# A depthwise convolution's band weights: two loads of the same rows, or one load and a ScalarE copy across partitions

## The chip, the cores and the metric

The program runs on one NeuronCore of a Trainium2 chip. The metric is the device time of one launch in microseconds (us), as a median over runs. PE is TensorE, PEld its weight loads, DVE is VectorE, ACT is ScalarE, POOL is GpSimd and SP is SyncE, which here only issues DMAs.

## The reference

Two layers act on an image batch `x` of 32 x 128 x 56 x 56 (images, channels, rows, columns), all in float32. Layer 0 is a ConvNeXt-like block with routed experts; layer 1 treats the pixels as tokens and does an attention within each token and a second routed feed-forward. Cut to what matters here, layer 0 begins with

```python
x = jax.lax.conv_general_dilated(input, dw_kernel, (1, 1), ((3, 3), (3, 3)),
        feature_group_count=C, dimension_numbers=('NCHW', 'OIHW', 'NCHW')) + dw_bias[None, :, None, None]
x = jnp.transpose(x, (0, 2, 3, 1))
...                      # layer norm over the channels, router, top 2 of 8 experts, expert MLPs
return input + x_skip + moe_out
```

So each channel is convolved with its own 7 x 7 kernel. The change touches only this first step. Everything behind it (router, selection, experts, the token attention, the second feed-forward) is the same in both kernels.

## The kernel before, in words

**The convolution as matmuls.** For one channel and one column offset `kw`, the 7 vertical taps are a banded 56 x 56 matrix that maps input rows to output rows. The kernel puts image rows on partitions and does, for each of the 128 channels, 7 offsets `kw` x 4 matmuls of 64 x 64 quadrants of the PE array: the upper partitions (0 to 55) hold images 0 to 15, the lower ones (64 to 119) images 16 to 31, and each half is cut in two groups of 8 images. That makes 28 matmul instructions for a channel; the profile has two records for each, 56 in all (L241).

**The bands.** A padded copy of all kernels is written once to a tensor `band_d` in device memory (L208). For channel `c`, a DMA with overlapping rows (row step one element) reads 56 rows of 728 elements of it into the tile `band` (L225). This is done twice, once for the upper and once for the lower partitions (`r` = 0, 1), with the same source. DVE then copies the 56 useful columns of each of the 7 offsets in reversed order into `br` (L235), over all 128 partitions. `br` holds the weights that the matmuls use: the upper half for `r = 0`, the lower half for `r = 1`. `band`, `br` and the input tile `xin` each have three buffers that channels take in turn, so the buffers of channel `c` are written again for channel `c + 3`.

**In and out.** Two DMAs on SP's queue load the channel's images into `xin` (L231). The results of the two halves stand in two PSUM tiles `cps`, of which there are four (two channels). ACT takes the first one out with a bias into `ot` (L253), DVE the second (L255), and four DMAs on ACT's queue store them to `conv_d` (L258). `ot` has four buffers, again two channels.

**What sets the order.** The kernel is written as a plain loop over channels. The framework orders the instructions of each engine's queue by its own estimate, and an engine runs its queue in that order. Eight semaphores are dealt out in turn to the DMAs of SP and ACT together; before a DMA is issued, its queue waits for the DMA that had the same semaphore before. In this kernel a channel has 8 such DMAs (2 `xin`, 2 `band`, 4 stores), so each of them gets the semaphore of its own kind of the channel before.

At the start a few small copies for the next stage stand among the convolution's instructions: in DVE's queue, `raw<-wg` (L342), which waits for the load of the router's weights `wg` (L333, issued by SP), stands between `br` of channel 5 and `ot` of channel 3. The next stage, the router, begins with loads of `conv_d` into `ct` (L358) and matmuls `pc<-jm,ct` (L364).

Of the kernel before, what the change touches and what calls it, by code (L numbers as in the profile page):

```python
# [20 lines left out]
KS = 7  # L21
# [4 lines left out]
def conv_attn_hybrid_kernel(  # L26
# [24 lines left out]
    nc = tc.nc  # L51
    N, C, H, W = x.shape
# [34 lines left out]
    band_d = dram.tile([C, KS * 2 * H], F32, name="band_d")  # L87
# [107 lines left out]
    HP = P // 2  # L195
    NB = NK // 2
    BL = (KS - 1) * 2 * H + H
    assert H <= HP and NK % 2 == 0 and NB * W * 4 <= 2048
    with tc.tile_pool(name="cv_c", bufs=1) as cc, tc.tile_pool(
        name="cv", bufs=3  # L200
    ) as cv, tc.tile_pool(name="cv_p", bufs=4, space=PSUM) as cvp:
        wt = cc.tile([C, KS, KS], F32, name="wt")
        nc.sync.dma_start(wt.rearrange("c a b -> c (a b)"), dw_kernel.rearrange("c o a b -> c (o a b)"))
        gp = cc.tile([C, KS, 2 * H], F32, name="gp")
        nc.vector.memset(gp, 0.0)
        for kh in range(KS):
            nc.vector.tensor_copy(gp[:, :, H - 1 - PAD + kh], wt[:, kh, :])
        nc.sync.dma_start(band_d, gp.rearrange("c a b -> c (a b)"))  # L208
        bias = cc.tile([P, C], F32, name="bias")
        nc.sync.dma_start(bias, dw_bias.partition_broadcast(P))  # L210

        nbuf = 3
        bands = [cc.tile([P, KS, 2 * H], F32, name=f"band{i}") for i in range(nbuf)]
        turned_bands = [cc.tile([P, KS, HP], F32, name=f"br{i}") for i in range(nbuf)]
        xins = [cc.tile([P, NK, WP], F32, name=f"xin{i}") for i in range(nbuf)]
        for i in range(nbuf):
            nc.vector.memset(bands[i], 0.0)
            nc.vector.memset(turned_bands[i], 0.0)
            nc.gpsimd.memset(xins[i], 0.0)
        cview = conv_d.rearrange("n c (h w) -> c h n w", w=W)  # L220
        for c in range(C):
            bt, br, xi = bands[c % nbuf], turned_bands[c % nbuf], xins[c % nbuf]
            for r in range(2):
                rows = slice(r * HP, r * HP + H)
                nc.sync.dma_start(  # L225
                    bt[rows].rearrange("p a b -> p (a b)")[:, :BL],
                    bass.AP(
                        band_d.tensor, band_d.offset + c * KS * 2 * H, [[1, H], [1, BL]]
                    ),
                )  # L230
                nc.sync.dma_start(  # L231
                    xi[rows, :, PAD : PAD + W],
                    x[r * NK : (r + 1) * NK, c].rearrange("n h w -> h n w"),
                )
            nc.vector.tensor_copy(br[:, :, :H], bt[:, :, :H][:, :, ::-1])  # L235
            pss = [cvp.tile([P, NB, W], F32, name="cps") for r in range(2)]
            for kw in range(KS):
                for r in range(2):
                    rows = slice(r * HP, r * HP + H)
                    for b in range(2):  # L240
                        nc.tensor.matmul(  # L241
                            pss[r][b * HP : (b + 1) * HP],
                            br[rows, kw, :],
                            xi[rows, b * NB : (b + 1) * NB, kw : kw + W],
                            start=(kw == 0),
                            stop=(kw == KS - 1),
                            tile_position=(r * HP, b * HP),
                            skip_group_check=True,
                        )
            for r in range(2):  # L250
                ot = cv.tile([P, NB, W], F32, name="ot", bufs=4)
                if r == 0:
                    nc.scalar.activation(ot, pss[r], AF.Identity, bias=bias[:, c : c + 1])  # L253
                else:
                    nc.vector.tensor_scalar(ot, pss[r], bias[:, c : c + 1], None, ALU.add)  # L255
                for b in range(2):
                    n0 = r * NK + b * NB
                    nc.scalar.dma_start(  # L258
                        cview[c][:, n0 : n0 + NB, :], ot[b * HP : b * HP + H]
                    )  # L260
# [553 lines left out]
    with tc.tile_pool(name="ex_w", bufs=2) as ew, tc.tile_pool(  # L814
# [42 lines left out]
        for i, (e, b) in enumerate(blocks):  # L857
# [15 lines left out]
            xa, rows, n = got.pop(i)  # L873
# [607 lines left out]
    with tc.tile_pool(name="f_c", bufs=1) as cc, tc.tile_pool(  # L1481
# [6 lines left out]
        rows = cc.tile([E2, FF2], F32, name="hbr")  # L1488
# [110 lines left out]
```

## Time and profile before

| | |
|---|---|
| median of 3 runs | 9506.17 us (9501.17 to 9524.23) |
| the profiled execution's own time | 9507.39 us |
| its span, first to last instruction | 9505.7 us |
| mean granted TensorE clock | 0.945 |
| the convolution's matmuls (L241), first and last start | 11.1 us and 700.6 us |
| their records, and the mean of one | 7168, 541 ns |
| DVE copy `br<-band` | 128 x 381 ns |
| ACT `ot<-cps` / DVE `ot<-cps` | 128 x 633 ns / 128 x 683 ns |
| bytes of one DMA: `xin`, `band`, store to `conv_d` | 196.0, 159.2, 98.0 KB |

The span is 1.7 us shorter than the execution's own time. A busy time is the sum of an engine's instruction durations; four quadrant matmuls run beside each other, so the 541 ns of one record is not the pace of the PE. An instruction's idle time is put down to what released it last. DMA issues and semaphore waits on a queue are not busy time of the engine, but the engine behind the queue can do nothing else meanwhile.

### The profile page before, as it was taken

To read this page: it belongs to the slowest core of one execution; us is meant where nothing else is said; L and a number is where in the kernel's file an instruction comes from. 1 tells how busy PE (TensorE), PEld (TensorE's weight loads), DVE (VectorE), ACT (ScalarE), POOL (GpSimd) and SP (SyncE) were. 2 spreads that over 40 slices of the span, in tenths; PEclk is the share of its full clock that TensorE was granted. 3 is DMA by queue.
4 is the path that set the end of the run, shared out by engine and by line. 5 is a ranking of instruction groups with operands and counts; after the bars stand their busy time and mean duration, and the time that the engine had idled before them with its cause. 6 is when DMAs were issued, how large, how long until landed. Compare 5 with 4: busy or idle time off the path is not lost. (4 is left out here: it accounts for less than half of the span.)

```text
span 9505.7 us, 165321 instructions
## 1 busy us (share of the span) xinstructions
PE 8565.6 (90%) x62216; PEld 6983.3 (73%) x62216; DVE 6481.0 (68%) x10957; ACT 5277.1 (56%) x13401; POOL 6777.5 (71%) x4884
## 2 busy tenths in 40 slices
PE   9999558775999999998999999999999999999878
PEld 3459546554766666666889899988989988989733
DVE  1117889885222222225999999999999999999623
ACT  1116644332333333334788888888888888888600
POOL 0002137777787777777999999999999999999500
PEclk9999779998999999999999999999999999999865
DMA  9994238775444444442000000000000000000199
GB/s 205 213 205 142 70 103 226 209 210 150 77 62 71 71 69 69 70 65 39 25 31 31 31 28 26 29 31 31 31 31 25 29 30 31 31 31 31 62 317 336
DMA packets 996146, 849.92 MB, mean 89 GB/s; under 512 B 525013, under 2 KB 880664, under 8 KB 975859
## 3 DMA queue, kind: packets, MB, share of 16 engines
q1 hardware_dynamic: 470162, 494.25, 18.6%
q0 software_dynamic: 177664, 188.81, 11.5%
q10 hardware_dynamic: 347520, 156.28, 6.1%
q8 instruction: 493, 8.08, 0.4%
q14 instruction: 307, 2.51, 0.1%
HBM read 486.34 MB, written 353.64 MB: 88 GB/s over the span
## 5 line engine op out<-in xcount | busy, mean ns | idle before, releaser
L161 POOL TENSOR_TENSOR s<-s,q 128x2048 f32<-128x2048 f32 x784 | 3601.9, 4605 | 137.8 <-DVE s L161 107.5
L161 ACT ACTIVATE s<-s 128x2048 f32<-128x2048 f32 x784 | 1500.8, 1914 | 685.9 <-POOL s L161 682.2
L161 POOL DMA_INDIRECT t_d<-ys,xe x992 | 1530.5, 1543 | 409.2 <-issue 229.0
L161 DVE TENSOR_TENSOR s<-kv,c 128x2048 f32<-128x2048 f32 x784 | 1786.5, 2279 | 8.0 <-POOL c L161 8.0
L161 DVE TENSOR_TENSOR ev<-s,kv 128x2048 f32<-128x2048 f32 x784 | 1784.0, 2276 | 2.4 <-ACT s L161 2.4
L161 PE MATMUL sm<-ident,ev 128*128 128x128 f32 x12544 | 1530.6, 276 | 45.4 <-DVE ev L161 45.4
L161 PE MATMUL sm<-ident,s 128*128 128x128 f32 x12544 | 1526.1, 275 | 8.5 <-ACT s L161 8.5
L161 PEld LDWEIGHTS sm<-ident,ev 128*128 128x128 f32 x12544 | 1436.3, 144 | 92.8 <-DVE ev L161 50.6
L161 PEld LDWEIGHTS sm<-ident,s 128*128 128x128 f32 x12544 | 1405.0, 143 | 20.8 <-ACT s L161 8.7
L888 ACT ACTIVATE hT<-ph,b1t 128x512 f32<-128x512 f32 (+1 forms) x992 | 679.3, 685 | 1236.5 <-PE ph L884 1220.8
L899 DVE TENSOR_TENSOR ys<-py,b2t 128x512 f32<-128x512 f32 (+1 forms) x248 | 171.4, 691 | 1545.9 <-PE py L894 1454.2
L894 PEld LDWEIGHTS py<-w,hT 128*128 128x128 f32 x7936 | 960.6, 192 | 202.1 <-issue 91.5
L894 PE MATMUL py<-w,hT 128*128 128x128 f32 x7936 | 984.6, 278 | 0.2
L884 PE MATMUL ph<-xeT,w 128*128 128x512 f32 (+1 forms) x1984 | 921.3, 597 | 69.5 <-DVE xeT L880 69.5
L697 POOL DMA_INDIRECT xb_d<-xs,rd x784 | 766.5, 978 | 240.2 <-issue 199.2
L241 PE MATMUL cps<-xin,br 56*64 56x448 f32 x7168 | 687.5, 541 | 13.6 <-DVE br L235 11.1
L884 PEld LDWEIGHTS ph<-xeT,w 128*128 128x128 f32 x1984 | 348.3, 190 | 392.0 <-issue 293.2
L241 PEld LDWEIGHTS cps<-xin,br 56*64 56x64 f32 x7168 | 334.0, 132 | 366.4 <-issue 331.2
L161 PE MATMUL pa<-rw,ct 128*128 128x256 f32 x1568 | 393.4, 393 | 127.6 <-DVE xs L161 127.5
L287 POOL MEMSET code<- 128x64 f32 x1 | 0.2, 151 | 697.4 <-DMA conv_d<-ot 697.4
L161 PEld LDWEIGHTS pa<-rw,ct 128*128 128x128 f32 x1568 | 283.7, 194 | 261.0 <-DVE xs L161 172.0
L161 PE MATMUL kv<-wq,zT 128*128 128x256 f32 x1568 | 417.2, 389 | 52.7 <-DVE ev L161 52.3
(330 smaller groups left out, 13264.5 us busy)
## 6 DMA issues: line engine op xcount, KB each, us to landing
ct<-conv_d SPq DMA_DIRECT2D x192, 448.0 KB
xin<-in_x_dram SPq DMA_DIRECT2D x256, 196.0 KB
conv_d<-ot ACTq DMA_DIRECT2D x512, 98.0 KB
t_d<-xs ACTq DMA_DIRECT2D x112, 448.0 KB
tr<-t_d SPq DMA_DIRECT2D x112, 448.0 KB
to<-t_d SPq DMA_DIRECT2D x32, 1568.0 KB
out_dram<-oo ACTq DMA_DIRECT2D x32, 1568.0 KB
xg<-in_x_dram SPq DMA_DIRECT2D x96, 448.0 KB
```

What stands on the lines that cost most here:

```text
L161: r = getattr(self.engine, name)(*a, **k)
L241: nc.tensor.matmul(pss[r][b * HP : (b + 1) * HP], br[rows, kw, :], xi[rows, b * NB : (b + 1) * NB, kw : kw + W], start=(kw == 0), stop=(kw ...
L287: nc.gpsimd.memset(code, -1.0)
L697: s = nc.gpsimd.indirect_dma_start(out=xb_d, out_offset=bass.IndirectOffsetOnAxis(ap=idx, axis=0), in_=row, in_offset=None, bounds_check=R ...
L884: nc.tensor.matmul(ph[:, :, :rows], w1[:, f * P : (f + 1) * P], xT[:, :, :rows], start=True, stop=True,)
L888: nc.scalar.activation(hT[:, f, :, :rows], ph[:, :, :rows], AF.Gelu, bias=b1t[:, f : f + 1])
L894: nc.tensor.matmul(py[:rows, j, :], hT[:, f, j, :rows], w2[:, f, :], start=(f == 0), stop=(f == NF - 1),)
L899: nc.vector.tensor_tensor(ys[:rows], py[:rows], across(b2t, SB)[:rows], ALU.add)
```

## The change

One band load for a channel instead of two, into the upper partitions alone. DVE reverses the upper half alone (56 partitions). ACT then copies the finished weights from the upper to the lower partitions of `br`.

```diff
         for c in range(C):
             bt, br, xi = bands[c % nbuf], turned_bands[c % nbuf], xins[c % nbuf]
+            nc.sync.dma_start(
+                bt[:H].rearrange("p a b -> p (a b)")[:, :BL],
+                bass.AP(band_d.tensor, band_d.offset + c * KS * 2 * H, [[1, H], [1, BL]]),
+            )
             for r in range(2):
                 rows = slice(r * HP, r * HP + H)
                 nc.sync.dma_start(
-                    bt[rows].rearrange("p a b -> p (a b)")[:, :BL],
-                    bass.AP(
-                        band_d.tensor, band_d.offset + c * KS * 2 * H, [[1, H], [1, BL]]
-                    ),
-                )
-                nc.sync.dma_start(
                     xi[rows, :, PAD : PAD + W],
                     x[r * NK : (r + 1) * NK, c].rearrange("n h w -> h n w"),
                 )
-            nc.vector.tensor_copy(br[:, :, :H], bt[:, :, :H][:, :, ::-1])
+            nc.vector.tensor_copy(br[:H, :, :H], bt[:H, :, :H][:, :, ::-1])
+            nc.scalar.copy(br[HP : HP + H, :, :H], br[:H, :, :H])
```

In the built program the new copy for channel `c + 3` stands in ACT's queue behind `ot` of channel `c` and its four stores, and ahead of `ot` of channel `c + 1`. In DVE's queue `br` of channel `c + 3` now stands ahead of `ot` of channel `c` instead of behind it. With seven DMAs for a channel, the eight semaphores no longer fall on the same kind of DMA in each channel. `raw<-wg` stands two channels earlier in DVE's queue, ahead of `ot` of channel 1, and SP issues the load of `wg` sooner. From the router on, each engine's instructions stand in the same order as before.

## The prediction

> **What bounds the kernel now.** The change touches only the convolution, so I read first when that stage runs and which engine sets its pace: the busy time by stretches, for the matmul line L241 alone. The columns are time, PE busy with its records, PEld busy with its records, granted clock, DMA share, GB/s.
>
> ```profile
> 0.00:50.00 50.00, 37.09 (x344) 14.88 (x348) 0.97 0.88 180
> 50.00:100.00 50.00, 50.00 (x532) 19.95 (x528) 1.00 1.05 213
> ...
> 250.00:300.00 50.00, 49.73 (x520) 22.11 (x516) 1.00 1.01 211
> 300.00:400.00 100.00, 99.57 (x1048) 47.74 (x1044) 1.00 1.04 215
> 400.00:500.00 100.00, 100.00 (x1056) 44.52 (x1052) 1.00 1.03 214
> 500.00:600.00 100.00, 100.00 (x1058) 72.79 (x1054) 1.00 1.04 213
> 600.00:700.00 100.00, 100.00 (x1056) 52.09 (x1048) 1.00 0.96 197
> ```
>
> Two things are full at once. PE runs 1056 records in 100 us at full clock; a channel has 56, so it takes 56 / 1056 x 100 = 5.30 us. The DMA engines show a share near 1.0: a channel moves 2 x 196.0 + 2 x 159.2 + 4 x 98.0 = 1102.4 KB, which at 213 GB/s takes also 5.30 us. Which one leads? In the last row the DMA rate falls to 197 GB/s and the record count stays 1056, so PE has a pace of its own. In the rows of 250 to 400 us the count falls a little (520 against 530 or so, 1048 against 1056): there DMA led for moments.
>
> All 128 channels at 5.30 us are 679 us. From the first matmul (11.1 us) to the end of the last (701.1 us) are 690. So about 11 us of the stage are not PE's pace: that is all that an edit to the feeding can remove behind the first matmul. The second view, who waited for whom up to 700 us, says why PE is so rarely held although the other engines wait all the time:
>
> ```profile
> PE cps L241 <- DVE br L235: 11.1, 1, 11.1
> PE cps L241 <- DVE ot L255: 1.8, 1, 1.8
> PE cps L241 <- DMA xin<-in_x_dram: 0.6, 3, 0.3
> ...
> ACT ot L253 <- DMA conv_d<-ot: 372.2, 79, 6.0
> ACT ot L253 <- PE cps L241: 224.4, 46, 13.3
> ```
>
> PE waited for the first weights (11.1 us), once for an eviction, and almost never for images. ACT waited 372 us for stores; that is slack, as long as it ends before PE needs the PSUM tile two channels on. The one long hold is on DVE, in the timeline at the start of the stage (start, duration, engine, line, and in brackets the idle time before):
>
> ```profile
> 33.38 0.39 DVE L235 COPY br<-band 128x392 f32<-128x392 f32 x1 [2.88 <-DMA band<-band_d]
> 42.03 0.17 DVE L342 COPY raw<-wg 128x8 f32<-128x8 f32 x1 [8.26 <-DMA wg<-in_L_conv_Wg_dram]
> 42.15 0.68 DVE L255 TENSOR_SCALAR ot<-cps,bias 128x448 f32<-128x448 f32 x1
> ```
>
> DVE stood 8.3 us for the router's small weight load; the eviction of channel 3 came behind it, and channel 5 could not go on. PE lost 2.3 us between two groups of matmuls, and in the 4 us after that the granted clock reads 0.57; channel 5 took 9.4 us instead of 5.3, so the hold costs 4.1 us.
>
> A rule on this can be set beside it: the Trainium skill, "TensorE: Matmul & The Clock Gate", Part 1, has the clock halve after an idle window of about 3.4 us. Here a hold of some 2.3 us was followed by a low clock, so the row decides; by the rule alone the hold would cost 2.3.
>
> **The change part by part**, against the profiled execution's own 9507.39 us (1.2 us above the median).
>
> *Removed: one `band` load a channel.* 128 x 159.2 KB and 128 issues of about 0.39 us on SP. At 213 GB/s it is 0.77 us of DMA time a channel, 98 us in all, but PE's 5.30 us stay, so what is won is only where DMA made PE late after start-up: the small holds between 250 and 370 us. The starts of the channels there are 0.3, 0.25, 0.16, 0.40, 0.59 and 0.40 us late: 2.1 us. I take -2.1; the bounds are -2.1 and 0.
>
> *Changed: DVE's reversal on 56 partitions.* Still 392 elements for a partition, so still 0.38 us: nothing. It now stands ahead of DVE's `ot` of three channels before. Both wait for the same channel of PE, and the band has landed long before (SP issues it right after the reversal three channels earlier, some 16 us ahead). So `ot` moves by 0.4 us with two channels of slack: nothing.
>
> *Added: 128 ACT copies, 56 x 392, SBUF to SBUF.* No row has this form. Near ones are the 448-element eviction at 0.633 us and the `pk<-m` copy of 14 elements out of SBUF at 0.198; on the line between them 392 elements take 0.58 us. The bounds are 0.46 (the fastest 384-element copy from PSUM) and 0.69 (the 512-element ACTIVATE); the eviction is the nearest row, so I take 0.58, with 0.1 for each handover.
>
> A price in the skill, "VectorE: DVE Perf Modes", section on the TRN2 errata, speaks against many small ScalarE copies out of SBUF (224 cycles before the first element) and gives (224 + 392) / 1.2 GHz = 0.51 us, as an estimate; only if all copies lay in the open would the sum differ, by 128 x 0.07 = 9 us.
>
> Where does it lie? Behind the four stores of channel c, ahead of `ot` of channel c + 1. This is ACT's queue where DMA was late, and where it was not (the ACTq rows are the stores' issues with the waits between them):
>
> ```profile
> 249.56 4.49 ACTq L258 DMA_DIRECT2D conv_d<-ot  x4
> 254.10 0.63 ACT L253 ACTIVATE ot<-cps,bias 128x448 f32<-128x448 f32 x1 [5.11 <-DMA conv_d<-ot]
> 255.27 4.80 ACTq L258 DMA_DIRECT2D conv_d<-ot  x4
> ```
> ```profile
> 150.40 0.63 ACT L253 ACTIVATE ot<-cps,bias 128x448 f32<-128x448 f32 x1 [4.68 <-PE cps L241]
> 151.06 3.84 ACTq L258 DMA_DIRECT2D conv_d<-ot  x4
> 155.72 0.63 ACT L253 ACTIVATE ot<-cps,bias 128x448 f32<-128x448 f32 x1 [4.68 <-DMA conv_d<-ot]
> ```
>
> In the easy stretch the last store is issued 4.4 us after PE ended the channel, and ACT is then free for 0.8 us (154.90 to 155.72): the copy of 0.58 and a handover fit. In the late stretch the last store goes out up to 7.5 us after PE's end. The copy then ends at 7.5 + 0.1 + 0.58 + 0.1 = 8.3 us, and PE starts channel c + 3 two channels after that end, at 10.6. It is hidden with 2.3 us to spare even there, and the next eviction comes 0.7 us later with the same two channels of slack. Nothing on the path; if the cover were gone it would be 0.68 a channel, 87 us.
>
> *The semaphores.* Each DMA still waits for the one eight back, which is now one channel and one DMA back. Stores wait in part for loads and the other way round. With eight DMAs in flight and seven for a channel, the round trip may take 8 / 7 x 5.30 = 6.1 us instead of 5.3 before PE feels it. Nothing, or the small gain counted above.
>
> *Start.* The second band load of channel 0 was issued 0.39 us after the first and is gone; the copy and a handover (0.68) come before the first lower matmul. +0.3; bounds -0.4 and +0.7.
>
> *The wait for `wg`.* The load stands earlier on SP, behind the band load that follows DVE's reversal for channel 3 (about 19.5 us). Issued by some 22 us and landed 3.8 us after that, as before (38.2 to 42.0), it is there at about 26; DVE's `ot` of channel 1 behind it is needed only when PE starts channel 3, at 29.5. So the hold goes: -4.1. If the loads ahead on SP make it 4 us later, a like hold comes two channels earlier: 0.
>
> *Behind the stage* the order is the same and the first `ct` load waits for the last stores; all of it moves with the end.
>
> Sum: -2.1 + 0.3 - 4.1 = -5.9 us, and 9507.39 - 5.9 = 9501.5; on the median, 9500.3. I forecast 9500. That is 0.06%; a measurement of this kernel tells about 0.3% (28 us) from no change.
>
> **Rivals.** *ACT's queue becomes the bound (slower).* In the late stretch `ot` to `ot` on ACT is already 5.5 to 6.0 us, with nothing in it but the eviction and the stores' waits. If these waits do not shrink when a load is gone, a copy of 0.58 with its handover makes the loop 0.68 longer. It decides once the loop is over 5.30 us for many channels in a row. In the some 30 channels from 205 to 370 us alone: 30 x 0.68 = 20 us, 9526. In all 128: 87 us, 9593. For it: 372 us of ACT's waits are for stores. Against it: these waits last as long as transfers are in flight, and 14% of the bytes go; most channels outside that stretch have ACT waiting for PE.
>
> *DMA was the bound underneath (faster).* If the equal 5.30 us of DMA were what paced PE, a channel would fall towards 4.53 us: up to 98 us, 9408. Against it: the count of records did not move between 197 and 215 GB/s, and PE's records stand without idle time. Even with every hold gone the stage ends 11 us sooner: 9495, no measurable gain.
>
> *The edit's gains do not show:* `wg` is late again and the late stretch stays. Then only the start's 0.3 is left: 9506 on the median.
>
> **How the numbers follow.** My forecast, and the rivals that end within 28 us of it (holds all gone, holds all kept, ACT's loop late in one stretch): 0.80. ACT's loop as the bound over most channels, 34 us and more: 0.12. DMA as the hidden bound, or a stage behind that gains from it: 0.08. The range takes in 9495, 9506 and 9526, with the 0.1 to 0.2% by which the runs of before differ: 9482 to 9534.
>
> **What would show it.** Right: 1056 records in every 100 us of the stage at full clock, its last matmul near 695 us, DMA under 200 GB/s, no 8 us wait on DVE, ACT copies of about 0.58 us, none of them named as releaser of PE but the first. Wrong: PE idle before `cps` with ACT `br` as releaser in many channels, or more than 1060 records in 100 us, or a time under 9478 or over 9535.

## The result and the profile after

| | before | after |
|---|---|---|
| median | 9505.73 us (12 runs, 9491.51 to 9524.23) | 9505.41 us (12 runs, 9496.33 to 9508.58) |
| ratio, 95% interval | | 0.9998 [0.999, 1.0005] |
| own time / span of the profiled execution | 9507.39 / 9505.7 us | 9507.5 / 9505.8 us |
| first convolution matmul; start of the last | 11.1; 700.6 us | 10.2; 692.2 us |
| first router matmul | 707.2 us | 699.0 us |

The time is the same, as forecast. The convolution itself ended 8 us sooner, and these 8 us are not in the total: both halves of that need an explanation.

The busy time of the matmul line by stretches (time, PE busy with its records, PEld busy with its records, granted clock, DMA share, GB/s), of the kernel after, where the matmul is L240:

```profile
50.00:100.00 50.00, 50.00 (x532) 34.43 (x528) 1.00 0.89 183
250.00:300.00 50.00, 50.00 (x532) 34.27 (x528) 1.00 0.89 185
300.00:400.00 100.00, 100.00 (x1058) 68.35 (x1054) 1.00 0.88 184
600.00:700.00 100.00, 92.77 (x978) 62.95 (x970) 0.98 0.82 172
```

The records are as many as before (532 and 1058 against 532 and 1048): PE's pace did not move. DMA's share fell from 1.04 to 0.88, and the dip of 250 to 400 us is gone. The last row holds fewer matmuls because the stage ends in it.

Who waited for whom up to 700 us, in the profile after (total us, times, longest):

```profile
ACT br L234 <- DMA conv_d<-ot: 286.8, 123, 4.5
ACT ot L252 <- PE cps L240: 200.6, 105, 4.7
PE cps L240 <- DVE br L233: 10.2, 1, 10.2
DVE raw L341 <- DMA wg<-in_L_conv_Wg_dram: 3.0, 1, 3.0
```

PE waits once, for the first weights. The old wait of ACT's eviction for the stores now stands in front of the new copy, 287 us instead of 372, and the eviction behind it has become early: it waits for PE in 105 channels instead of 46. DVE's wait for `wg` is 3.0 us instead of 8.3. In ACT's timeline a channel looks so (start, duration, and in brackets the idle time before):

```profile
150.48 0.64 ACT L252 ACTIVATE ot<-cps,bias 128x448 f32<-128x448 f32 x1 [1.90 <-PE cps L240]
151.15 3.16 ACTq L257 DMA_DIRECT2D conv_d<-ot  x4
154.35 0.52 ACT L234 COPY br<-br 56x392 f32<-56x392 f32 x1 [3.23 <-DMA conv_d<-ot]
155.80 0.63 ACT L252 ACTIVATE ot<-cps,bias 128x448 f32<-128x448 f32 x1 [0.93 <-PE cps L240]
```

Even in this late channel the copy is done at 154.87 and ACT then stands idle for 0.93 us until PE ends the next channel.

**Where the 8 us went.** Landmarks of the two profiled executions can be subtracted (after minus before): -8.2 us at the first router matmul, -5.8 at 1344 us where the scatter stage behind the router starts, -8.5 at 4430 us, -8.2 still at 8950 us, -2.6 at 9125 us where the output stage starts, and +0.1 at the end; between the router and 8950 it swings from -4.7 to -10.3. More than half of the loss (4.5 us) falls within 25 us behind 8950. This is the same stretch of work there, before and then after (time, busy time of PE, PEld, DVE, ACT, POOL, granted clock, DMA share, GB/s):

```profile
8962.00:8975.00 13.00, 5.52 (x49) 4.74 (x48) 4.20 (x5) 9.22 (x26) 0.81 (x4) 0.78 0.05 20
```
```profile
8953.80:8971.30 17.50, 10.07 (x49) 9.04 (x49) 4.16 (x5) 9.39 (x26) 0.81 (x4) 0.60 0.03 10
```

The same 49 matmuls on the path took 5.52 us at a mean clock of 0.78 and 10.07 us at 0.60: the clock fell at the start of the stretch in the second execution, and 7.3 us into it in the first. The remaining 2.7 us were lost in the output stage, whose length lies between 375.8 and 385.1 us in the profiles of this case, whatever the kernel. Whether such losses belong to the change or to chance is the first question for the runs.

### The profile page after: what moved, and what is told of

Its sections match the earlier page's. It is cut to its first block, busy times and chain, and to the rows that moved or that the text cites. A ratio compares the mean times of both kernels' runs of the same rounds, so it can differ in the third digit from the quotient of the medians.

```text
span 9505.8 us, 165442 instructions
## 1 busy us (share of the span) xinstructions
PE 8560.7 (90%) x62216; PEld 7114.1 (75%) x62216; DVE 6472.3 (68%) x10957; ACT 5347.6 (56%) x13529; POOL 6781.0 (71%) x4884
## 3 DMA queue, kind: packets, MB, share of 16 engines
q1 hardware_dynamic: 461202, 473.37, 17.4%
## 5 line engine op out<-in xcount | busy, mean ns | idle before, releaser
L240 PE MATMUL cps<-xin,br 56*64 56x448 f32 x7168 | 682.6, 539 | 10.2 <-DVE br L233 10.2
L240 PEld LDWEIGHTS cps<-xin,br 56*64 56x64 f32 x7168 | 466.8, 132 | 225.2 <-issue 11.2
```

The lines of the kernel that those rows point to most:

```text
L240: nc.tensor.matmul(pss[r][b * HP : (b + 1) * HP], br[rows, kw, :], xi[rows, b * NB : (b + 1) * NB, kw : kw + W], start=(kw == 0), stop=(kw ...
```

## The experiments

Theory A: PE has a pace of its own in this stage, the copy is hidden behind it, the change takes some 8 us of holds away, and the total doesn't show them because later stages vary by more. Theory B: something later in the program answers to the change and gives the 8 us back. Against A stood also the rivals of the prediction (ACT's loop as the bound, DMA as the hidden bound).

Four runs (`r_after`, `r_before`, `e_wg_pool`, `e_two_loads`) were on another chip, where the kernel before takes 9922.13 us (27 runs; the scatter stage behind the router takes 1420 us there instead of 1004); they are compared within that chip. The others ran on two chips like the first, beside 13 and 21 runs of the kernel before with medians of 9507.7 and 9507.8.

### The pair again, and the kernel before against itself

No edit: the changed kernel twice (`r_after`, `r_after2`), the kernel before once.

> The changed kernel once more, unaltered, for the spread of each stage. Theory A (the gain is real and small): the convolution's last matmul again starts near 692 us and the router's first near 699, 8 us sooner than before, to within 1 us; what the total shows is set by stages behind it that vary by several us from run to run, so the median lies 0 to 8 us under the one before. Theory B (the change makes a later stage slower): the time from the first router matmul to the end is longer by the same 8 us in each profile of this kernel.

> The kernel before once more, unaltered, against itself. Both theories: the last matmul of the convolution near 700 us, the channel-5 hold of about 4 us there again. Theory A: the time from the first router matmul (about 707 us) to the end differs by 3 us or more from the first profile's 8798.5 us in one direction or the other. Theory B: it agrees within 1 us.

> The changed kernel a third time, unaltered. If the stage's 8 us reach the end, the ratio to the kernel before lies at 0.9991 within its interval, and the time from the first router matmul to the end differs from profile to profile by more than 8 us, so one pair of profiles cannot show it. If the gain is given back behind, the ratio lies at 1.0000 or over and that time is 8 us longer than in the kernel before on the same chip.

Measured: `r_after` 9913.12 us, ratio 0.9992 [0.9983, 1.0001]; `r_after2` 9500.71, 0.9993 [0.9984, 1.0002]; the kernel before against itself 9914.93, 0.9996 [0.9987, 1.0005]. The gain of the stage came back each time: the first router matmul stood at 698.98 us in `r_after2` (707.20 before). On the other chip it is smaller, 699.49 against 704.70, so 5.2 us where 8 to within 1 were expected.

What follows, from that matmul to the end of the span, took 8798.5 us in the profile before and 8806.8 in the one after, but 8800.0 in `r_after2`; in other profiles on such chips it was 8793.8 and 8794.5 in two kernels with the changed convolution (eight and four copies) and 8807.1 in one with the old order (`e_both_read`, below). On the other chip it was 9210.4 in the kernel before, 9217.0 in the kernel after and 9203.9 in `e_wg_pool`, which has the old convolution. So it varies by 13 us with no regard to the change: theory B falls. (The comparison of `r_before` with the first profile's 8798.5 says nothing, as the chips differ.)

The 8 us are 0.09%, and none of the three intervals of the changed kernel shows them by itself. Nor do the medians: `e_both_read`, whose convolution ended 1 us later than before, has the same ratio of 0.9993 as `r_after2`.

### The hold for `wg` alone

The kernel before, with the router's small copy off DVE's queue:

```diff
-        nc.vector.tensor_copy(raw[:, C + C :], wg)
+        nc.gpsimd.tensor_copy(raw[:, C + C :], wg)
```

> The kernel before with only the small copy of the router's weights moved from DVE to POOL, both band loads kept. If the 8 us wait on DVE for that load is what held channel 5, PE has no hold there and the stage's last matmul starts at 696 us (700 - 4.1), the late stretch between 250 and 370 us stays (2 to 3 us). If the hold came from the images or the band loads, it stays, and the last matmul starts at 700.

Measured: 9917.4 us, 1.0002 [0.9992, 1.0011]. PE's timeline up to 60 us, of `r_before` on the same chip and of this kernel:

```profile
43.37 17.09 PE L241 MATMUL cps<-xin,br 56*64 56x448 f32 x160 [2.14 <-DVE ot L255]
```
```profile
10.45 49.99 PE L241 MATMUL cps<-xin,br 56*64 56x448 f32 x496 [10.45 <-DVE br L235]
```

Channel 5 was no longer late (4.43 us in `r_before`), and the last matmul started at 694.6 instead of 698.4. So the hold is worth the 4 us that the prediction gave it, the gain can be had without the change, and the time doesn't show it.

### The copy alone, with all that the change removes put back

The kernel before, where ACT writes the lower half once more:

```diff
             nc.vector.tensor_copy(br[:, :, :H], bt[:, :, :H][:, :, ::-1])
+            nc.scalar.copy(br[HP : HP + H, :, :H], br[:H, :, :H])
```

> The kernel before with both band loads and DVE's reversal of both halves kept, and ACT's copy put on top (it writes the lower weights once more). This is the copy alone, without the relief for DMA. Theory A (hidden: two channels of slack on ACT even where the stores are late): last matmul of the convolution between 692 and 704 us, no PE wait for ACT's copy. Rival (ACT's queue becomes the bound when the stores' waits do not shrink): the copy makes ACT's loop 0.6 us longer wherever stores are late, last matmul at 710 us or later.

Measured: 9504.74 us, 0.9993 [0.9984, 1.0003], last matmul at 701.6 us. Rows of its profile, the waits up to 700 us and two stretches of the matmuls (L242 there):

```profile
ACT br L236 <- DMA conv_d<-ot: 400.9, 117, 5.5
PE cps L242 <- DVE ot L256: 2.3, 1, 2.3
PE cps L242 <- DMA xin<-in_x_dram: 1.2, 5, 0.3
```
```profile
200.00:250.00 50.00, 48.81 (x500) 21.29 (x496) 1.00 1.08 202
```
```profile
300.00:400.00 100.00, 100.00 (x1058) 66.41 (x1054) 1.00 1.03 213
```

With both loads in place, DMA at 1.03 and 401 us of ACT's waits for stores ahead of the copies, PE still runs 1058 records from 300 to 400 us. The prediction's slow rival needed just this: waits that stay while the copy comes on top. It had 20 us for the late stretch alone and 87 in all, and neither came, so the copy is hidden without help from the removed load.

It is not shown to be free to the last us. Thirteen channels between 180 and 260 us took 0.2 to 0.5 us longer than the others and three near the end 0.1 to 0.3: 5.6 us in all, where the kernel before lost 2.1 so. PE's waits there name the images and never the copy, and `r_before` lost nothing of this kind, so one profile can't say whether the copy has a part in it.

The hold for `wg` is in this run too, but the granted clock stayed at 1.00 behind it: channel 5 lost 2.9 us and not 4.1.

An earlier attempt at the same question put a second band load back into the changed kernel, with nobody reading the lower half:

```diff
-            nc.sync.dma_start(
-                bt[:H].rearrange("p a b -> p (a b)")[:, :BL],
-                bass.AP(band_d.tensor, band_d.offset + c * KS * 2 * H, [[1, H], [1, BL]]),
-            )
+            for r in range(2):
+                nc.sync.dma_start(
+                    bt[r * HP : r * HP + H].rearrange("p a b -> p (a b)")[:, :BL],
+                    bass.AP(band_d.tensor, band_d.offset + c * KS * 2 * H, [[1, H], [1, BL]]),
+                )
```

> The changed kernel, but the band is again loaded for both halves (the lower half is not read; ACT's copy makes the lower weights as in the changed kernel). Theory A (DMA load makes the late stretch; ACT's copy is hidden even then): holds of some us come back, the last matmul between 694 and 705 us. Rival (ACT's queue is the bound once the stores' waits are as long as before): ACT's loop gets 0.6 us longer in every late channel, the last matmul at 715 us or later.

Measured: 10002.3 us, 1.0088 [1.0073, 1.0104], last matmul at 774.5 us. By the number that is the rival's (715 or later), but the mechanism is neither theory's: no wait of PE's matmuls names ACT. Its busy times by stretches (columns as in the wide rows above):

```profile
50.00:100.00 50.00, 44.73 (x360) 18.36 (x364) 6.89 (x13) 6.90 (x12) 0.00 (x0) 0.86 0.96 207
...
300.00:400.00 100.00, 100.00 (x1060) 39.17 (x1056) 20.29 (x38) 21.34 (x37) 0.00 (x0) 1.00 0.92 184
```

PE's waits from 50 to 300 us have this at their head:

```profile
PE cps L241 <- DMA xin<-in_x_dram: 27.8, 33, 2.5
```

Channels 6 to 37 took some 7.9 us each, partly by these waits and partly because the granted clock was 0.83 to 0.93 up to 300 us. From then on PE ran at its old pace, with 184 GB/s as in the changed kernel. SP's queue shows band loads in bunches of up to five: ahead of the images of channel 30 stood 134 of them where the kernel before has 66, ahead of those of channel 40 171, and from there on one more for each channel. So by channel 40 the loads that nobody reads had run through to the last of the 128, ahead of images that PE needed. The run says nothing on the copy; it shows that a load without a reader is not a neutral weight to add.

### How much of the copy fits

The changed kernel with the copy four and eight times:

```diff
-            nc.scalar.copy(br[HP : HP + H, :, :H], br[:H, :, :H])
+            for _ in range(8):
+                nc.scalar.copy(br[HP : HP + H, :, :H], br[:H, :, :H])
```

> The changed kernel with ACT's copy done four times over for each channel. In the changed kernel ACT is done with a channel's eviction, stores and copy about 3.5 us after PE ended the channel and then free for about 2 us; three more copies of 0.52 are 1.55 us. Theory (the copy is hidden with room): last matmul of the convolution still near 692 us, time unchanged. Rival (anything put into ACT's queue shows): 3 x 0.52 x 128 = 198 us later.

> The changed kernel with ACT's copy done eight times over. Seven more copies are 3.6 us and no longer fit into the 2 us that are free. Theory: ACT's queue becomes the bound with a loop of 0.65 (eviction) + 1.5 to 2.4 (stores) + 4.1 (copies) = 6.3 to 7.1 us a channel instead of 5.31, the stage 125 to 230 us longer, and PE names ACT's copy or eviction as releaser. If PE still does not wait, the loop was reckoned wrong.

Measured: four copies 9499.93 us, 0.9992 [0.9982, 1.0002], PE at 5.31 us a channel, last matmul at 696.1; channel 0 alone is clearly longer (10.5 us instead of 7.2). Eight copies 9728.87 us, 1.0235 [1.0218, 1.0252], 7.01 us a channel in the median, last matmul at 925.1, which is 233 us later than with one copy (125 to 230 were expected). One channel of the eight, PE and ACT in the timeline:

```profile
299.54 0.63 ACT L253 ACTIVATE ot<-cps,bias 128x448 f32<-128x448 f32 x1
300.20 1.88 ACTq L258 DMA_DIRECT2D conv_d<-ot  x4
300.23 5.66 PE L241 MATMUL cps<-xin,br 56*64 56x448 f32 x56 [1.32 <-ACT ot L253]
302.13 4.36 ACT L235 COPY br<-br 56x392 f32<-56x392 f32 x8 [1.96 <-DMA conv_d<-ot]
306.52 0.63 ACT L253 ACTIVATE ot<-cps,bias 128x448 f32<-128x448 f32 x1
```

ACT's loop is closed without a gap: eviction 0.63, the stores' issues and their waits 1.9, copies 4.4, together 7.0 us from 299.54 to 306.52, and PE now waits for the eviction, 1.32 us here and in nearly every channel alike. That is the slow rival's mechanism in full, and it needs a loop over 5.30 us. With one copy the same sum is about 0.63 + 1.9 + 0.52 = 3.1 us where the stores' waits are as short as here, which leaves room for four copies and not for eight.

### Is DMA the bound underneath?

Leaving out kernel offsets takes work from PE alone, so DMA must show itself if it stands close below. First with four offsets, in both kernels:

```diff
-            for kw in range(KS):
+            for kw in range(0, KS, 2):
```

> The kernel before with 4 of the 7 column offsets (3 are left out, so the stages behind get other data and only the convolution's time is read). PE needs 4/7 x 5.31 = 3.04 us a channel. Theory (DMA stands close under PE): the stage is then paced by DMA at 5.0 to 5.3 us a channel, 640 to 690 us, hardly shorter than with seven offsets. Rival (DMA has much room): it follows PE to 3.1 to 3.5 us a channel, 400 to 450 us.

> The changed kernel with 4 of the 7 column offsets, read like the one before it. Theory (DMA stands close under PE, and the removed load is 14% of its bytes): 4.3 to 4.6 us a channel, 550 to 600 us, so here the change is worth 60 to 100 us. Rival (DMA has much room): the same as the kernel before with four offsets. Second rival (waits on ACT's queue, not bytes, pace it): not faster than the kernel before with four offsets.

Measured (one run each): 10033.23 us for the kernel before with less work, 9.5 us a channel, and 9516.45 us for the kernel after, 5.47 us a channel. Both miss what either theory expected. The kernel before with four offsets, PE and DVE in the timeline:

```profile
302.02 9.25 PE L241 MATMUL cps<-xin,br 56*64 56x448 f32 x32 [1.13 <-issue]
```
```profile
300.94 0.68 DVE L255 TENSOR_SCALAR ot<-cps,bias 128x448 f32<-128x448 f32 x1 [9.41 <-PE cps L241]
301.54 0.38 DVE L235 COPY br<-band 128x392 f32<-128x392 f32 x1
```

The framework had ordered DVE's queue anew: the reversal for the next channel now stands behind the eviction of the channel that PE is just ending, so PE stops for 1.13 us in every channel. And the 32 matmuls behind a stop take up to 9.25 us, because the granted clock is low (columns as in the rows of the matmul line above):

```profile
200.00:250.00 50.00, 44.33 (x178) 15.13 (x172) 0.57 0.57 115
```

The kernel after with four offsets has lost the order of its original too, and its clock was 0.80 to 0.95 from 100 to 700 us, so the pair is not a comparison. The stop alone does not explain the clock. With eight copies PE stopped for 1.32 us in every 7.0, and this is its row:

```profile
200.00:300.00 100.00, 80.56 (x784) 48.17 (x784) 0.98 0.73 139
```

What kept the clock low with four offsets stays open.

"TensorE: Matmul & The Clock Gate", Part 1, of the Trainium skill gives an idle window of about 3.4 us for the clock to halve and a busy one of the same length for it to return. By that rule a stop of 1.13 us is too short to halve the clock, and 9.25 us of unbroken work are long enough to bring it back. The row of the eight copies agrees; the row of the four offsets says otherwise, and the row decides.

Then with six offsets, where the queues keep the order of their originals:

```diff
-            for kw in range(KS):
+            for kw in range(KS - 1):
...
-                            stop=(kw == KS - 1),
+                            stop=(kw == KS - 2),
```

> The kernel before with 6 of the 7 column offsets (one is left out; the stages behind get other data, so the convolution's time alone is read). The queues' order in the steady stage is that of the kernel before. PE needs 6/7 x 5.31 = 4.56 us a channel. Theory (DMA stands right under PE: 1102 KB a channel at 205 to 215 GB/s): DMA paces it at 5.2 to 5.5 us a channel, about as long as with seven offsets, 680 to 715 us. Rival (DMA has room): 4.6 us, 595 to 605 us.

> The changed kernel with 6 of the 7 column offsets, read like the one before it. Theory: 943 KB a channel at 205 to 215 GB/s are 4.5 to 4.7 us, so PE's 4.56 leads or nearly: 590 to 620 us, and the change is worth 70 to 110 us here. Rival (no masking; the change never saves more than the stage's 8 us): 5 to 15 us shorter than the kernel before with six offsets.

Measured (one run each): 9472.52 us for the kernel before with six offsets, last matmul at 666.4 us, 5.06 us a channel in the median and 5.13 in the mean; 9475.08 us for the kernel after, 660.1 us, 4.84 and 5.08. PE's own pace would be 6/7 x 5.30 = 4.54, the stage then about 97 us shorter; it got 34 and 32 us shorter. So in the kernel before, what feeds PE (DMA, with the waits of its queues) stood only some 0.2 us a channel below PE. The stage's end at 666 us lies between the theory (680 to 715) and the rival (595 to 605); the kernel after is 6.3 us sooner, as the rival without masking had it (5 to 15), and far from the theory's 70 to 110. The stretch and SP's two largest waits, of the kernel before with six offsets:

```profile
100.00:200.00 100.00, 96.27 (x966) 42.87 (x960) 1.00 1.04 230
```
```profile
SPq L231 <- DMA xin<-in_x_dram: 161.5, 184, 2.3
SPq L225 <- DMA band<-band_d: 116.0, 124, 2.1
```

and of the kernel after with six:

```profile
100.00:200.00 100.00, 95.57 (x964) 42.35 (x956) 0.98 1.09 192
```
```profile
SPq L223 <- DMA conv_d<-ot: 196.3, 99, 3.4
SPq L229 <- DMA conv_d<-ot: 167.9, 106, 3.0
```

The records are the same but for two, at 230 GB/s and at 192: 14% of the bytes are gone, and the pace isn't faster. By bytes, the load was worth 0.77 us of DMA time a channel. What came through is 0.22 us in the median and 0.05 in the mean. Three things can hold the rest back.

One is packets: each channel still moves 3584 packets of 224 bytes (images and stores), and only 56 packets of 2912 bytes went. In the trace of the kernel before with six offsets, from 100 to 600 us, a band packet took 146 ns in the mean, an image packet 19.2 and a store packet 17.8. At that price a band load is 56 x 146 / 16 = 0.51 us of the 16 engines and not 0.77.

The second is that this price did not hold. The stores' queue from 100 to 600 us, with six offsets before and after (packets, MB, share of 16 engines' time):

```profile
q10 hardware_dynamic: 183307, 39.84, 40.2%
```
```profile
q10 hardware_dynamic: 182245, 39.61, 47.3%
```

As many store packets took 17.5 ns each before and 20.8 after, and an image packet went from 19.2 to 22.1. For 3584 packets on 16 engines that is 0.69 us a channel more, which is over the 0.51 of the band load. (Packet times overlap, as the shares over 1 in the rows above show.)

The third is the semaphores: with seven DMAs for a channel, SP's loads wait for landings of stores (364 of 500 us), where before they waited for loads. No run here separates these, or shows why the packets got slower.

A rule of the Trainium skill bears on the packets: "DMA: Bandwidth & Descriptors", "Why small descriptors are slow", adds about 3 cycles to a packet's 32-byte beats. By it (an estimate) the ratio of a band packet to a small one is (91 + 3) / (7 + 3) = 9.4; the trace's mean times in the loads' queue give 146 / 19.2 = 7.6.

## Why the prediction was right

The forecast (9500, the same within 0.3%) stands: 9505.41, and 0.9992 and 0.9993 in the repeats against a forecast ratio of 0.9994. The total could not have told this forecast from one of no gain at all; what tests it is the stage. The steps, one by one:

- **PE's own pace of 5.30 us.** Right: 1058 records at DMA shares of 1.03 and 0.88 alike, 5.31 with four copies. The equal 5.30 us that the prediction worked out for DMA showed nothing, though: 213 GB/s is what the stage moved at PE's pace, and with six offsets the kernel before moved 224 (100 to 600 us).
- **The copy is hidden.** Right, and shown with both loads in place. Its length was mis-sized: 0.517 us measured, 0.58 on the line between two rows. "VectorE: DVE Perf Modes" of the Trainium skill had 0.51 as an estimate, and the trace agrees with it. The spare was put at 2.3 us in the worst channels; it is larger: from channel 3 on, the copy ended at least 4.7 us before PE started its channel, and the last store went out at most 4.8 us after PE's end, where up to 7.5 had been reckoned (one late channel of the kernel before reached over 8). With both loads in place the spare was at least 3.2 us.
- **The wait for `wg`, -4.1.** Right: `wg` landed by 26.4 us (26 was forecast; it was issued later than reckoned, at 23.7 instead of 22, and landed faster, so two errors cancel), DVE's eviction of channel 1 came late within its slack, and channel 5 lost nothing; the POOL kernel shows the same on its own. Judging by `e_both_read`, which had the hold without the low clock behind it, some 1.2 us of the 4.1 are that clock.
- **The late stretch, -2.1.** Right: the lateness outside start and channel 5 went from 2.1 us to none. On the other chip the kernel before had no such stretch, and `e_both_read` had 5.6 us, so this term changes from profile to profile.
- **The start, +0.3.** This term was wrong in sign in this pair. The first matmul came at 10.20 instead of 11.13 us and channel 0 took 7.2 instead of 7.8: -1.5 us together. The prediction laid all of the copy on the path; in the trace DVE's first reversal started at 9.71 instead of 10.63 us, and the first lower matmul, behind the copy, at 10.70. How much of it is the change is open: channel 1 started at 17.4 to 17.8 us in three profiles of the changed kernel, and at 17.6 to 19.0 in four with both loads.
- **The semaphores cost nothing.** Right at PE's pace. The six-offset pair shows that they do tie loads to stores once DMA is near the bound.
- **The sum.** -5.9 was forecast for the stage, -8.2 to -8.4 measured; 1.8 of the difference is the start, and the rest is spread over the channels in amounts under 0.1 us. On the total it is -0.3 in one comparison and about -7 in another, all inside the intervals: the 13 us by which the stages behind vary swallow it.
- **The rivals.** ACT's loop as the bound: its threshold is real and lies between four and eight copies. DMA as the hidden bound: it lies some 0.2 us a channel below PE, and the price by bytes (4.53 us a channel without the load) was too good; with six offsets, where PE needs 4.54, the channel took 4.84 in the median and 5.08 in the mean.

No kernel run here with the whole convolution is measurably faster than either.

## What to carry to other kernels

Ask which engine would set the pace if the edit made everything else free; if the count of its records is the same in stretches with different DMA rates, bytes saved beside it are worth only the holds that can be named one by one. An added instruction on an engine that waits for PE is free until the engine's whole loop is longer than PE's channel: add up that loop, with the queue's waits in it, rather than the instruction. Do not cost a removed transfer by its bytes at the rate of the stage alone: look at the times of the packets that stay, before and after, and at which transfers share semaphores when the number of transfers in a loop changes.

## What the runs showed of the hardware that was not expected

- With a stop of 1.13 us in every channel TensorE's mean granted clock stayed at 0.57, so that four offsets took longer (9.5 us a channel) than seven at full clock (5.30); with a stop of 1.32 us in every 7.0 another kernel kept 0.98. What makes the difference is not shown.
- A stretch of 49 matmuls late in the program took 5.52 or 10.07 us by where the clock fell, 4.5 us on the path from one execution to the next.
- One chip was 4% slower on this kernel than those of the other runs, nearly all of it in one stage of indirect transfers (1004 against 1420 us), with the convolution alike within 3 us.
- The same pace of matmuls came with 230 and with 192 GB/s when the bytes that went were in few large packets; the small packets that stayed took 17.5 ns each before and 20.8 after.
